# Adding the output projection to x with ScalarE and POOL instead of VectorE in a four-layer RWKV and graph-convolution kernel

## The chip, the cores and the metric

The kernel runs on one core of a Trainium2 chip. The metric is the device time of one execution, in microseconds (us). A profile is one execution recorded by the hardware profiler; its span is the time from the first to the last recorded instruction. Engines are named as in the profile: PE is TensorE (matrix products), DVE is VectorE, ACT is ScalarE, POOL is GpSimd, and SP is SyncE, whose queue issues the large transfers between HBM and SBUF here.

## The reference

x has 16 images of 192 channels and 56 x 56 points, in fp32. Three layers of a bidirectional RWKV mixer and one graph convolution follow each other, each on a group-normalised x and each added to x:

```
for layer in 0, 1, 2:                     # T = 3136 points, C = 192 channels
    xs = group_norm(x)                    # 32 groups, over 6 channels and all points
    k, v, r = xs @ Wk.T, xs @ Wv.T, xs @ Wr.T
    x_bi = 0.5 * (wkv(k, v) + flip(wkv(flip(k), flip(v))))
    h = sigmoid(r) * x_bi
    h = (h - mean(h)) * rsqrt(var(h) + 1e-5) * ln_g + ln_b     # over the channels
    x = x + h @ Wo.T
x_j = max(0, x shifted by 2 points in each of four directions, less x)      # on group_norm(x)
x = x + gelu(batch_norm([x, x_j] @ conv_w.T + conv_b))
```

wkv is a scan over the points: per channel, p becomes decay * p + exp(k) * v and q becomes decay * q + exp(k), and the output is (p + c * exp(k) * v) / (q + c * exp(k)). The group norm of the next layer needs the sum and the sum of squares of the new x over all points, before the first product of that layer.

## The kernel before, in words

Two images make a pair: 2 x 192 channels stand in three columns j = 0, 2, 1 of 128 partitions. A tile of one chunk is 128 x 3 x 448 (448 of the 3136 points, so 7 chunks). There are eight pairs in two streams of four. While one stream runs its backward scan and its output (the functions `b_...`), the other runs the forward scan of its layer (`a_...`) or the graph convolution (`c_...`). A table of 249 steps says which units meet: `both_a` (85 steps) and `both_a_first` (17) join a backward chunk b with a forward chunk a, `both_c` (42) a backward chunk with a convolution chunk, `forward_a` (66), `forward_c` (14), `backward_alone` (24) and `neither` (1) have one or none.

There is no scheduler: within a step each function writes its instructions, and each engine carries out its own in the order in which they were written. `nback` and `nfront` are the chunks of the next step, whose r and k products and exponentials are begun a step early. The output of a backward chunk is spread over two or three steps: `late` holds the chunks that are not finished and how far they are, and l is such a chunk.

One chunk of `both_a` in its parts, with the lines of the profile:

- `b_q`, `b_p`, `a_q`, `a_p`: three scans each on VectorE (L836). Their decays lie in PSUM. `save` copies the last column for the next chunk, q's on ACT (L845), p's on POOL (L847).
- `b_den`, `b_num`, `a_den`, `a_num`: the bonus c * exp(k) added to the state, two VectorE operations each (L851), both inputs in SBUF.
- `a_ekv`: exp(k) * v from v's product in PSUM (L885). `b_scale`: h times the inverse deviation from PSUM (L1014). `b_rs2`: the variance (L997).
- `invert`: 1 / q as exp(-ln q) on ACT (L906, L909); `b_sigmoid` likewise (L941, L909); `b_exp`, `a_exp` (L934, L866) take the exponentials out of PSUM.
- `b_mix`: nine POOL operations (L969 to L971) that form h. `a_y`: one POOL product over the whole chunk (L913), into the tile that the backward pass of that layer adds to.
- `b_squares` (L978), `b_sums` (PE, `st`), `b_rs1`, `b_rs3` (L993, L1002, L1003), `b_spread` (PE, `rsb`): the deviation over the channels.
- `b_out`: the output product, `ops` in PSUM. `b_x`: adds it and a column `wob` to x in SBUF, three VectorE operations (L1027), and sends x to HBM through SP's queue (L1029).
- `b_stats`, called by `sum_up`: per column j one pass on ACT for the sum and one for the sum of squares of the new x (L722, L723). With the last chunk (c = 0) the next layer begins: its `norm_sums` (L728), `norm_var` and `norm_fold` come at the next calls of `gap()`.

PSUM has seven banks for products, taken and returned in turn (`bank`, `release`); a product waits until the last reader of its banks is done. SBUF has 33 chunk slots, also taken in turn. SP's queue carries, in the written order, the loads of the next chunks (`load_ahead`), the stores of the convolution's result (`store`) and the stores of x.

Of the kernel before, what the change touches and what calls it, by code (L numbers as in the profile page):

```python
# [39 lines left out]
P = 128  # L40
# [433 lines left out]
def fast_path(ctx: ExitStack, tc: tile.TileContext, flag, x, wproj, wfold, wcfold, wconst, wgroup, sums, picks, vecs, out):  # L474
# [7 lines left out]
    keep = ctx.enter_context(tc.tile_pool(name="fkeep", bufs=1))  # L482
    row = ctx.enter_context(tc.tile_pool(name="frow", bufs=1))
    small = ctx.enter_context(tc.tile_pool(name="fsmall", bufs=4))
    dram = ctx.enter_context(tc.tile_pool(name="fdram", bufs=1, space=bass.MemoryType.DRAM))
    psum = ctx.enter_context(tc.tile_pool(name="fpsum", bufs=1, space=bass.MemoryType.PSUM))
    psconst = ctx.enter_context(tc.tile_pool(name="fpsconst", bufs=1, space=bass.MemoryType.PSUM))
# [217 lines left out]
    class Run:  # L705
        def __init__(self, pr, l, stats, src=None, first=None):
            self.pr, self.l, self.stats, self.src = pr, l, stats, src
            self.xa, self.xb, self.xz = {}, {}, {}
            if first is not None:
                self.xa[0] = first  # L710
            self.begun = False
            self.bias, self.carry, self.ps = {}, {}, {}
            self.ek, self.ekv, self.h, self.den, self.sg, self.rs = {}, {}, {}, {}, {}, {}
            self.m, self.ml, self.q, self.p = {}, {}, {}, {}

    def new_stats():
        return small.tile([P, 2, 3, NL], F32, tag="stats", name=name("stats"))

    def chunk_stats(stats, xt, c):

        for j in ORDER:
            S.activation(junk, xt[:, j, :], AF.Identity, accum_out=stats[:, 0, j, c : c + 1])  # L722
            S.activation(junk, xt[:, j, :], AF.Square, accum_out=stats[:, 1, j, c : c + 1])  # L723


# [115 lines left out]
    def save(run, key, s, col, eng=G):  # L841

        run.carry[key] = stile("c" + key)
        if key == "q":
            S.activation(run.carry[key], s.t[:, :, col : col + 1], AF.Copy)  # L845
        else:
            eng.tensor_copy(run.carry[key], s.t[:, :, col : col + 1])  # L847
# [167 lines left out]
            release(ps[j])  # L1015

    def b_out(run, c):
        h = run.h.pop(c)
        run.ps["o"] = banks("ops")
        project(run.ps["o"], params[run.l][5], of(h.t), L)  # L1020
        h.give()

    def b_x(run, c):
        wob, ps, xs = params[run.l][4], run.ps["o"], run.xb[c]
        for j in ORDER:
            xj = xs.t[:, j, :]
            V.scalar_tensor_tensor(xj, ps[j][:, 0:L], wob[:, column(j)], xj, ALU.add, ALU.add)  # L1027
            release(ps[j])
        nc.sync.dma_start(run.dst[c], xs.t)  # L1029

    def b_stats(run, c):
        xs = run.xb.pop(c)
        chunk_stats(run.new, xs.t, c)
        if c == 0:
            require_all(run.chk, slice(0, NCHK))
            nxt = run.follow
            nxt.stats, nxt.src = run.new, run.dst
            nxt.xa[0] = xs
            begin_later(nxt)
        else:  # L1040
            xs.give()
# [135 lines left out]

    late, unsummed = {}, []  # L1180

    def of_stage(n):
# [22 lines left out]
    def add(u):  # L1205
        b_x(*u)
        unsummed.append(u)
        del late[u]

    def keys(f):  # L1210
        if f is not None:
            begin_now(f[1])
# [11 lines left out]
    def both_a(b, a, nback, nfront):  # L1224
# [5 lines left out]
        store()  # L1230
        if nback is not None:
            b_gate(*nback[1:])
            b_exp(*nback[1:])
        b_q(*b)
        if l:
            b_rs2(*l)
            b_rs3(*l)
        b_sigmoid(*b)
        a_values(*a)
        if l:  # L1240
            b_spread(*l)
        b_p(*b)
        b_den(*b)
        invert(b[0].ek[b[1]])
        b_num(*b)
        b_mix(*b)
        if l:
            b_scale(*l)
            b_out(*l)
            late[l] = 2  # L1250
        a_ekv(*a)
        sum_up()
        keys(nfront)
        a_q(*a)
        if l:
            add(l)
        b_squares(*b, (0,))
        a_save(*a)
        exp_keys(nfront, (0, 2))
        b_squares(*b, (2,))  # L1260
        exp_keys(nfront, (1,))
        b_squares(*b, (1,))
        b_sums(*b)
        a_p(*a)
        gap()
        a_den(*a)
        b_rs1(*b)
        late[b] = 0.5
        invert(den())
        gap()  # L1270
        a_num(*a)
        a_y(*a)
        gap()

    def both_a_first(b, a, nback, nfront):

# [89 lines left out]
    def forward_a(a, nback, nfront):  # L1366
# [10 lines left out]
        if l and late[l] == 0:  # L1377
            squares_and_sums(l)
            b_rs1(*l)
            late[l] = 0.5  # L1380
        if l and late[l] == 0.5:
            b_rs2(*l)
            b_rs3(*l)
            late[l] = 1
        if l:
            b_spread(*l)
        elif ahead:
            keys(nfront)
        store()
        a_q(*a)  # L1390
        a_save(*a)
        if ahead and not l:
            exp_keys(nfront)
        a_den(*a)
        gap()
        invert(den())
        a_ekv(*a)
        gap()
        if l:
            b_scale(*l)  # L1400
            if ahead:
                keys(nfront)
                exp_keys(nfront)
            b_out(*l)
            late[l] = 2
        sum_up()
        if nback is not None:
            b_gate(*nback[1:])
        a_p(*a)
        gap()  # L1410
        if l:
            add(l)
            sum_up()
        a_num(*a)
        a_y(*a)
        if nback is not None:
            b_exp(*nback[1:])
# [235 lines left out]
```

## Time and profile before

| | before |
|---|---|
| runs, median (lowest to highest) | 5382.29 us (5372.49 to 5386.76), 3 runs |
| profiled execution, its time and its span | 5382.77 and 5381.0 us |
| busy PE, DVE, ACT, POOL | 4629.7, 5014.9, 3681.2, 2770.3 us |
| mean granted clock of PE | 0.916 |

Busy is the time in which an engine carried out at least one instruction. A group's row gives the line, the operation, out<-in by tile names, the shapes, how often, the busy sum and the mean of one in nanoseconds, then the idle time just before and what ended it. A row of the timeline gives start and duration in us of like instructions in a row; a duration holds the instruction's end as well, so three scans of 1.13 us follow each other at 1.05. `L836` is line 836 of the kernel before; the changed kernel's lines are some numbers higher.

### The profile page before, as it was taken

How to read it: one execution, taken by the hardware profiler on the slowest of the kernel's cores; microseconds unless marked ns; L12 is line 12 of the kernel's file. 1: busy time of each engine (PE TensorE's matmuls, PEld its weight loads, DVE VectorE, ACT ScalarE, POOL GpSimd, SP SyncE). 2: the span in 40 equal slices, each digit the busy share in tenths (PEclk: the TensorE clock that was granted, in tenths of full speed). 3: DMA queues.
4: the chain of work that ended last, by engine and by line, in shares of the span. 5: the costliest groups of instructions: out<-in, count | busy, mean ns of one | idle time of the engine just before them, and what ended most of it. 6: DMA issues, size and time to landing. Idle time of an engine off the chain costs nothing. (4 is left out here: it accounts for less than half of the span.)

```text
span 5381.0 us, 50984 instructions
## 1 busy us (share of the span) xinstructions
PE 4629.7 (86%) x15206; PEld 1498.6 (28%) x15206; DVE 5014.9 (93%) x6556; ACT 3681.2 (68%) x7035; POOL 2770.3 (51%) x2164
## 2 busy tenths in 40 slices
PE   6888988989798898888979888888888988898897
PEld 2222322223232222222323222222222222222222
DVE  6989999999999999999999999999999999999996
ACT  6777667767676676676667767667667566676673
POOL 1555555645454465555444455555535455555463
PEclk8989989989899898998989989999898998999898
DMA  5222212124243212213425121221343312222233
GB/s 149 78 80 72 85 66 88 63 90 140 87 131 89 82 63 73 74 67 105 144 87 150 56 74 67 85 74 62 111 139 94 111 56 74 70 77 80 77 102 115
DMA packets 314271, 482.42 MB, mean 90 GB/s; under 512 B 66432, under 2 KB 306688, under 8 KB 313984
## 3 DMA queue, kind: packets, MB, share of 16 engines
q1 hardware_dynamic: 312832, 477.59, 27.9%
q8 instruction: 123, 2.02, 0.2%
q10 hardware_dynamic: 1152, 1.48, 0.1%
q14 instruction: 164, 1.34, 0.1%
HBM read 324.83 MB, written 154.14 MB: 89 GB/s over the span
## 5 line engine op out<-in xcount | busy, mean ns | idle before, releaser
L913 POOL TENSOR_TENSOR p<-p,q 128x1344 f32<-128x1344 f32 x168 | 510.1, 3037 | 887.8 <-ACT q L909 472.1
L969 POOL TENSOR_TENSOR ekv<-ekv,ek 128x448 f32<-128x448 f32 x504 | 618.2, 1227 | 677.1 <-DVE p L1014 304.9
L836 DVE TENSOR_TENSOR_SCAN p<-fdecays,cp,ekv 128x448 f32<-128x448 f32 x864 | 928.5, 1130 | 7.2 <-POOL p L913 4.5
L836 DVE TENSOR_TENSOR_SCAN q<-fdecays,cq,ek 128x448 f32<-128x448 f32 x864 | 929.2, 1131 | 1.9 <-PE st L987 0.2
L971 POOL TENSOR_TENSOR p<-p,sg 128x448 f32<-128x448 f32 x504 | 599.4, 1189 | 54.5 <-ACT cq L845 10.7
L970 POOL TENSOR_TENSOR p<-p,ekv 128x448 f32<-128x448 f32 x504 | 600.6, 1192 | 39.5
L847 POOL COPY cp<-p 128x3 f32<-128x3 f32 x271 | 196.4, 725 | 686.9 <-DVE p L836 454.3
L978 ACT ACTIVATE ek<-p 128x448 f32<-128x448 f32 x504 | 283.6, 573 | 259.4 <-POOL p L971 257.5
L591 PE MATMUL ops<-p,fwo 128*128 128x448 f32 x336 | 223.5, 755 | 275.3 <-DVE p L1014 275.2
L866 ACT ACTIVATE ek<-k,k 128x448 f32<-128x448 f32 x504 | 292.1, 630 | 243.0 <-PE k L594 216.4
L723 ACT ACTIVATE fjunk<-x 128x448 f32<-128x448 f32 x672 | 387.6, 577 | 21.1
L722 ACT ACTIVATE fjunk<-x 128x448 f32<-128x448 f32 x672 | 384.6, 572 | 14.6
L851 DVE SCALAR_TENSOR_TENSOR q<-ek,fcc,q 128x896 f32<-128x896 f32 x336 | 337.1, 1043 | 51.1 <-ACT cq L845 51.1
L1009 PE MATMUL rsb<-rs,fpicks 32*128 32x448 f32 (+1 forms) x1008 | 335.8, 594 | 48.8 <-ACT rs L1003 46.7
L1027 DVE SCALAR_TENSOR_TENSOR x<-ops,fwob,x 128x448 f32<-128x448 f32 x504 | 315.9, 674 | 52.2 <-PE ops L594 27.1
L851 DVE SCALAR_TENSOR_TENSOR ek<-ek,fcc,q 128x896 f32<-128x896 f32 x336 | 361.6, 1117 | 2.8 <-POOL chk L919 2.8
L851 DVE SCALAR_TENSOR_TENSOR ekv<-ekv,fcc,p 128x896 f32<-128x896 f32 x336 | 330.4, 1024 | 1.2
L934 ACT ACTIVATE sg<-r,r 128x448 f32<-128x448 f32 x504 | 311.9, 624 | 15.8 <-PE r L594 10.4
L885 DVE SCALAR_TENSOR_TENSOR ekv<-v,v,ek 128x448 f32<-128x448 f32 x504 | 312.9, 677 | 0.0
L1014 DVE TENSOR_TENSOR p<-p,rsb 128x448 f32<-128x448 f32 x504 | 281.5, 614 | 31.1 <-PE rsb L1009 31.0
L851 DVE SCALAR_TENSOR_TENSOR p<-ekv,fcc,p 128x896 f32<-128x896 f32 x336 | 293.4, 913 | 10.0 <-POOL cp L847 9.7
L906 ACT ACTIVATE q<-q 128x1344 f32<-128x1344 f32 x168 | 222.4, 1324 | 90.4 <-DVE q L851 65.9
(232 smaller groups left out, 11795.3 us busy)
## 6 DMA issues: line engine op xcount, KB each, us to landing
x<-xd SPq DMA_DIRECT2D x240, 672.0 KB, 5.5
xd<-x SPq DMA_DIRECT2D x168, 672.0 KB, 4.0
x<-in_x_dram SPq DMA_DIRECT2D x320, 224.0 KB, 4.6
x<-in_x_dram SPq DMA_DIRECT2D x320, 112.0 KB, 4.6
out_dram<-ml SPq DMA_DIRECT2D x112, 224.0 KB, 2.3
ring<-xd SPq DMA_DIRECT2D x112, 168.0 KB, 5.3
wkv<-in_wfold_dram SPq DMA_DIRECT2D x24, 640.0 KB, 5.5
out_dram<-ml SPq DMA_DIRECT2D x112, 112.0 KB, 2.3
```

What stands on the lines that cost most here:

```text
L722: S.activation(junk, xt[:, j, :], AF.Identity, accum_out=stats[:, 0, j, c : c + 1])
L723: S.activation(junk, xt[:, j, :], AF.Square, accum_out=stats[:, 1, j, c : c + 1])
L836: V.tensor_tensor_scan(s.t[:, j, order], dec[:, column(j)].to_broadcast([P, L]), data.t[:, j, order], init, ALU.mult, ALU.add)
L851: by_channel(lambda js, i: V.scalar_tensor_tensor(dst.t[:, js, :], e.t[:, js, :], cc[:, i : i + 1], state.t[:, js, :], ALU.mult, ALU.add))
L885: V.scalar_tensor_tensor(e.t[:, j, :], ps[j][:, 0:L], b[:, j, :], run.ek[c].t[:, j, :], ALU.add, ALU.mult)
L913: G.tensor_mul(run.h[c].t, run.h[c].t, den.t)
L934: S.activation(sg.t[:, j, :], ps[j][:, 0:L], AF.Exp, bias=b[:, j, :], scale=-1.0, accum_out=run.chk[:, at : at + 1])
L969: G.tensor_mul(y.t[:, j, :], y.t[:, j, :], den.t[:, j, :])
L970: G.tensor_add(h.t[:, j, :], h.t[:, j, :], y.t[:, j, :])
L971: G.tensor_mul(h.t[:, j, :], h.t[:, j, :], sg.t[:, j, :])
L1009: PE.matmul(ps[j][:, :L], pick[rows, j, :], rs[rows, :], start=True, stop=True)
L1027: V.scalar_tensor_tensor(xj, ps[j][:, 0:L], wob[:, column(j)], xj, ALU.add, ALU.add)
```

## The change

In `both_a`, the output product of chunk l is no longer added to x by VectorE. ACT reads it from PSUM, adds `wob`, writes it over h and sums it by its accumulator (`b_evict`); POOL then adds h to x (`b_add`), behind `a_y`. As the accumulated sum is that of the addend alone, `whole_sums` adds the old x's sums, once for each run. Wherever VectorE still adds (`b_x`, all other steps), its operation writes the sum by an accumulator. So the pass for sums on ACT is gone everywhere and `b_stats` takes only squares. In `both_a` the state of p of chunk a is copied by ACT, the k product of the next chunk stands ahead of the output product, and `b_exp`, `a_q`, `a_ekv`, the squares and the Ln and Exp of den change places. `forward_a` with a chunk left over is put in another order too, with the output product ahead of k and `add` behind `a_num`. The statistics tiles get a pool of their own with seven buffers.

```diff
-    def chunk_stats(stats, xt, c):
-
-        for j in ORDER:
             S.activation(junk, xt[:, j, :], AF.Identity, accum_out=stats[:, 0, j, c : c + 1])
+        chunk_squares(stats, xt, c)
+
+    def chunk_squares(stats, xt, c):
+        for j in ORDER:
             S.activation(junk, xt[:, j, :], AF.Square, accum_out=stats[:, 1, j, c : c + 1])
...
-        if key == "q":
+        if key == "q" or eng is S:
             S.activation(run.carry[key], s.t[:, :, col : col + 1], AF.Copy)
...
     def b_x(run, c):
+        run.h.pop(c).give()
         wob, ps, xs = params[run.l][4], run.ps["o"], run.xb[c]
         for j in ORDER:
             xj = xs.t[:, j, :]
-            V.scalar_tensor_tensor(xj, ps[j][:, 0:L], wob[:, column(j)], xj, ALU.add, ALU.add)
+            V.scalar_tensor_tensor(
+                xj, ps[j][:, 0:L], wob[:, column(j)], xj, ALU.add, ALU.add, accum_out=run.new[:, 0, j, c : c + 1]
+            )
             release(ps[j])
         nc.sync.dma_start(run.dst[c], xs.t)
+    def b_evict(run, c):
+        wob, ps, h = params[run.l][4], run.ps["o"], run.h[c].t
+        for j in ORDER:
+            S.activation(
+                h[:, j, :], ps[j][:, 0:L], AF.Identity, bias=wob[:, column(j)], accum_out=run.new[:, 0, j, c : c + 1]
+            )
+            release(ps[j])
+    def b_add(run, c):
+        h, xs = run.h.pop(c), run.xb[c]
+        G.tensor_add(xs.t, xs.t, h.t)
+        h.give()
+        nc.sync.dma_start(run.dst[c], xs.t)
+        run.parts.append(c)
+    def whole_sums(run):
+        if run.parts:
+            cs = slice(min(run.parts), max(run.parts) + 1)
+            new = run.new[:, 0, :, cs]
+            G.tensor_add(new, new, run.stats[:, 0, :, cs])
     def b_stats(run, c):
         xs = run.xb.pop(c)
-        chunk_stats(run.new, xs.t, c)
+        chunk_squares(run.new, xs.t, c)
         if c == 0:
+            whole_sums(run)
...
     def both_a(b, a, nback, nfront):
         if nback is not None:
             b_gate(*nback[1:])
-            b_exp(*nback[1:])
         b_q(*b)
...
         invert(b[0].ek[b[1]])
+        if nback is not None:
+            b_exp(*nback[1:])
+        b_spread(*l)
         b_num(*b)
         b_mix(*b)
-        if l:
-            b_scale(*l)
-            b_out(*l)
-            late[l] = 2
+        a_q(*a)
+        a_save(*a)
         a_ekv(*a)
+        b_squares(*b, (0,))
         sum_up()
         keys(nfront)
-        a_q(*a)
-        if l:
-            add(l)
-        b_squares(*b, (0,))
-        a_save(*a)
-        exp_keys(nfront, (0, 2))
+        b_scale(*l)
+        b_out(*l)
         b_squares(*b, (2,))
-        exp_keys(nfront, (1,))
+        exp_keys(nfront)
+        a_p(*a, S)
         b_squares(*b, (1,))
-        b_sums(*b)
-        a_p(*a)
         gap()
         a_den(*a)
-        b_rs1(*b)
-        late[b] = 0.5
-        invert(den())
+        ln(den())
         gap()
         a_num(*a)
+        exp_minus(den())
+        b_sums(*b)
+        b_rs1(*b)
+        b_evict(*l)
         a_y(*a)
+        add_evicted(l)
         gap()
+        late[b] = 0.5
...
     def forward_a(a, nback, nfront):
+            b_spread(*l)
+            a_den(*a)
+            invert(den())
+            sum_up()
+            a_ekv(*a)
             b_scale(*l)
+            b_out(*l)
+            if nback is not None:
+                b_gate(*nback[1:])
             if ahead:
                 keys(nfront)
                 exp_keys(nfront)
-            b_out(*l)
-            late[l] = 2
-        sum_up()
-        if nback is not None:
-            b_gate(*nback[1:])
-        a_p(*a)
-        gap()
-        if l:
+            a_p(*a)
+            a_num(*a)
             add(l)
             sum_up()
```

## The prediction

> **What bounds the kernel now.** I read the busy table first, then the groups, then one step in the timeline, engine by engine.
>
> ```profile
> span 5381.0 us, 50984 instructions
> ...
> PE 4629.7 (86%) x15206; PEld 1498.6 (28%) x15206; DVE 5014.9 (93%) x6556; ACT 3681.2 (68%) x7035; POOL 2770.3 (51%) x2164
> ```
>
> VectorE (DVE) is nearly full, but that is a mean over seven kinds of step. Placing every instruction in its step (the program's order against the trace's, starts of VectorE's first instruction), the span holds 85 `both_a` steps (2171 us), 42 `both_c` (1045), 43 `forward_a` with no chunk left over (566), 17 `both_a_first` (507), 23 `forward_a` with one left over (449), 24 `backward_alone` (364) and others (213). The change acts on `both_a` first. They come in 17 rows of five, each row behind a `both_a_first`. Busy times of two neighbouring `both_a` steps (window, its length, then PE, PEld, DVE, ACT, POOL with counts, PE's granted clock, DMA share, GB/s), and from the timeline VectorE and POOL in the first (start, us, instruction):
>
> ```profile
> 426.59:451.91 25.32, 23.75 (x79) 7.52 (x78) 25.26 (x31) 19.13 (x36) 15.21 (x12) 0.93 0.27 83
> 451.91:477.23 25.32, 22.43 (x79) 6.94 (x78) 25.26 (x31) 19.18 (x36) 15.20 (x12) 1.00 0.23 81
> ```
>
> ```profile
> 433.65 1.72 DVE L851 SCALAR_TENSOR_TENSOR ek<-ek,fcc,q 128x896 f32<-128x896 f32 x2
> 435.29 1.74 DVE L851 SCALAR_TENSOR_TENSOR ekv<-ekv,fcc,p 128x896 f32<-128x896 f32 x2
> ...
> 443.46 1.84 DVE L1027 SCALAR_TENSOR_TENSOR x<-ops,fwob,x 128x448 f32<-128x448 f32 x3
> 445.22 3.23 DVE L836 TENSOR_TENSOR_SCAN p<-fdecays,cp,ekv 128x448 f32<-128x448 f32 x3
> 448.36 1.98 DVE L851 SCALAR_TENSOR_TENSOR q<-ek,fcc,q 128x896 f32<-128x896 f32 x2
> 450.25 1.74 DVE L851 SCALAR_TENSOR_TENSOR p<-ekv,fcc,p 128x896 f32<-128x896 f32 x2
> ```
>
> ```profile
> 428.56 3.04 POOL L913 TENSOR_TENSOR p<-p,q 128x1344 f32<-128x1344 f32 x1 [4.11 <-ACT q L909]
> ...
> 447.64 1.15 POOL L971 TENSOR_TENSOR p<-p,sg 128x448 f32<-128x448 f32 x1
> 448.73 1.06 POOL L847 COPY cp<-p 128x3 f32<-128x3 f32 x1
> 453.82 3.04 POOL L913 TENSOR_TENSOR p<-p,q 128x1344 f32<-128x1344 f32 x1 [4.03 <-ACT q L909]
> ```
>
> A step takes 25.32 us; VectorE works 25.26 of it, without a gap. But PE is at 22.4 us with the clock at 1.00 and 23.75 at 0.93, so it is close behind. ACT has 6 us to spare, POOL 10. And POOL's idle time is not free time. In a later `forward_a`, POOL's product and VectorE's two-input operation meet:
>
> ```profile
> 530.93 3.03 POOL L913 TENSOR_TENSOR p<-p,q 128x1344 f32<-128x1344 f32 x1 [5.11 <-ACT q L909]
> ...
> 532.36 3.15 DVE L851 SCALAR_TENSOR_TENSOR q<-ek,fcc,q 128x896 f32<-128x896 f32 x2 [0.32 <-ACT cq L845]
> ```
>
> The pair takes 1.72 us alone and 3.15 here: the 1.43 us more is the wait from 532.36 to about 0.2 before POOL's end at 533.96. The scans keep 1.13 us each under POOL's work.
>
> **What the skill says.** "SBUF — State Buffer", section "Who interferes with whom": a VectorE instruction with two SBUF inputs and a POOL instruction that reads SBUF exclude each other for the whole instruction, while one with a single SBUF input doesn't contend. The trace agrees (1.43 us above; `decays` is in PSUM, so a scan has one). "GPSIMD Engine Reference", "Engine selection": two-input elementwise work is about 2x slower there; the trace has 3.04 us on POOL against 1.6 on VectorE for 1344 columns (L1067). "TensorE: Matmul & The Clock Gate", Part 1: PE drops to half clock after an idle window of about 3.4 us; the trace has 0.93 and 1.00 in neighbouring steps. "VectorE: DVE Perf Modes", "Two Vector instructions with no wait between them": an operation with an accumulator output is two instructions; no row of this kernel has one on VectorE.
>
> **`both_a`, 85 steps.** VectorE loses L1027, 3 x 0.59 = 1.76 us from start to start, and the 0.25 us that `q` (1.98, not 1.72) waited for POOL: 25.3 - 2.0 = 23.3 us. ACT loses three sum passes (0.70 from start to start, 2.1 us) and gains three evictions (PSUM to SBUF with accumulator, as L934: 0.62 to 0.75, about 2.1 us) and one copy (0.2): nothing in sum, but the evictions stand at its tail and end about 4.1 us into the next step. Behind them on ACT wait the copy of q's state, rs3 and the sigmoid (0.2 + 1.3 + 2.7, until 8.3); Ln of ek is due at 8.8, so 0.5 us covers them, and each us beyond it would count in full. `b_exp`, moved behind Ln and Exp of ek, frees r's banks at 13.6 for rsb and k; `b_scale` wants rsb at 15.4: covered by 1 us. POOL loses one copy (1.06, mostly a wait) and gains one addition of 128x1344, taken as L913's 3.04 (L1094, the same form, has 3.17).
>
> Behind the addition on POOL stand the next copy of p and the mix at 11.6 us: not late. `whole_sums`, one small POOL operation in each of 24 runs (0.2 us by its 128x3 product, L919), ends long before `mv` is read, and the larger statistics pool moves no work: nothing for either.
>
> Now the order. The addition stands after L913, which waits for exp(-ln den), which is queued on ACT behind the last square, which waits for POOL's mix. Follow it with the trace's times from `b_den` at 433.65: `b_den`, Ln and Exp of ek, nine mix operations until 448.79: 15.14 us; square 0.61 (ends 449.40); Ln and Exp of den 2.71; hand-over and L913 0.14 + 3.04; addition 3.04, less 0.2 for the early release: 24.5 us. What comes then is the next step's `b_den`, which has two SBUF inputs and waits. On top of it, `a_den` now reaches VectorE 1.76 us earlier, at 20.0 us of the step, while the mix runs until 22.2: the last mix operation lets half of `a_den` (1.06) pass first and starts 0.7 to 1.0 later, and VectorE itself waits twice, 0.7 to 0.9 each. So a loop of 25.2 to 25.5 us takes the place of VectorE's 23.3.
>
> Two more loops end close by. PE: k 4.6, output product 4.6, st 2.2 (which formerly was not behind it), then rs1 0.6, rs2 0.65, `b_p` 3.15, two bonuses 3.3, `a_q` 3.15, two of `a_ekv` 1.2, which frees k's banks, and hand-overs 0.3: 23.7 us, with half clock in part of it (each such window costs 1.7) about 24.7. I also see PE left with only the short rsb products between v and k for some 4 us, no better than now for the clock. SP: the store now waits for the addition at 7.4 us of the next step, and that step's loads stand behind it in SP's queue:
>
> ```profile
> 445.33 0.56 SPq L1029 DMA_DIRECT2D xd<-x  x1
> 446.00 0.56 SPq L540 DMA_DIRECT2D x<-in_x_dram  x1
> ...
> 448.99 0.57 SPq L545 DMA_DIRECT2D x<-xd  x1
> ```
>
> Today they leave 18.7 us into the step before the one that uses them. After: 7.4 + 0.67 (store) + 0.67 (load for b) + 5.5 (median landing) = 14.2 us, against k's start at 14.9: hidden. In layer 0, b's load is four transfers (446.00 to 448.99, 3 us): 16.6 us, 1.7 late.
>
> The first `both_a` of a row of five has no addition ahead of it: 23.3 and the two waits at `a_den`, 24.7 to 24.8, -0.6. The other four: the first loop's middle, 25.35, and an estimated 0.2 for steps where half clock makes PE's loop the longer one: 25.55, +0.25 each (rounded up). Five steps: +0.4 us; x 12 rows = +5. Four layer-0 rows have about 2 late steps, +3.5 in all: 4 x 3.9 = +16. The row that also sums the input (28 to 29 us, ACT's chain, same load): 0.
>
> **`forward_a` with a chunk left over, then `backward_alone`.** 17 pairs follow a `both_a`. Loss: L913 and then the addition stand in front of `a_den`, which moved ahead: VectorE waits 0.1 + 2.9 us instead of 1.43; the output product starts 1.1 later than today. Gain: the next run's `mv` (VectorE waits 3.15 us for it until 553.8 in the first such step of layer 1) needs three passes on ACT after the last x, not six: -2.1. Net -1.0 x 17 = -17 us. The other six: 0.
>
> **Accumulators on VectorE.** The 83 chunks still added there get 249 reads. Nearest rows: VectorE's 128x1 and 128x3 copies, 0.065 to 0.2 from start to start; ACT's accumulator read, 0.19 a row. I take 0.15, bounds 0.05 and 0.3; no gain is possible from an added instruction. On the path: `both_c` (35 adds) and `both_a_first` (17), full of VectorE work: 156 x 0.15 = 23; `forward_a`, where VectorE waits for the product anyway (1.03 and 0.69), 5: +28 us (9 to 56). ACT's saved passes in `both_c` lie beside a gapless VectorE: 0; were they on its path, -2.1 x 35.
>
> **Sum.** +5 + 16 - 17 + 28 = +32 us on a span of 5381.0; that execution took 5382.77, the median of the runs is 5382.29: **5414 us**.
>
> **Rivals.**
> (B) The relief arrives: 24.3 us a step, VectorE's 23.3 and 1.0 of stalls. It decides if L913 and the addition are over when `b_den` comes at 7.05 us, that is, if exp(-ln den) ends by 0.95 + 0.2 us of the next step; by my loop it is 1.3, so 0.2 us a step decides, and a mix that starts 0.3 earlier would do it. For it: POOL's 10 idle us. Against: the chain above. 80 x -1.0 - 17 + 15 = -82: 5300 us.
> (C) SP's queue or the clock takes over: loads late in every row (landing 7 us instead of 5.5) or half clock in k's product each step: +0.9 x 68 + 16 + 28 - 17 = +88: 5470 us.
> (D) The parts cancel, reads at 0.05 and rows of layer 0 unharmed: +5 + 0 - 17 + 9 = -3: 5379 us, no change; what a measurement can tell here is about 0.3%, 16 us.
>
> **Chances.** Mine 0.45, B 0.25, C 0.14, D 0.16. Mine alone: 5390 to 5445 (reads 9 to 56, rows). The range 5310 to 5480 reaches into B and C until 2 in 10 are left out. Faster by over 0.3%: B and a tail of D, 0.28; within: 0.16; slower: 0.56.
>
> **What would show it.** Right: `both_a` steps of 25.2 to 25.8 us with VectorE gaps or stretched L851 rows (over 1.5 us in `ek` and `q`), the addition's row ending at 7 to 8 us of the next step, `mv` idle near 1 us. Wrong: `ek` rows of 1.13 us and steps under 24.5 (B); k's product waiting for a DMA in all rows (C); accumulator reads that fill no time. The weakest step is the loop of 25.2 to 25.5: 1% of it is 20 us.

## The result and the profile after

The changed kernel takes 5499.51 us (median; 5498.14 to 5501.03) against 5380.74 us before (5372.49 to 5386.76): a ratio of 1.0222, 95% interval 1.0204 to 1.024. The forecast was 5414 us, slower; the sign was right, but the loss is 119 us where 32 were forecast, and the time lies outside the range of 5310 to 5480.

The head of the changed kernel's page (span, then busy time, its share and the number of instructions of each engine):

```profile
span 5498.3 us, 50732 instructions
...
PE 4765.6 (87%) x15206; PEld 1535.6 (28%) x15206; DVE 5082.7 (92%) x6550; ACT 3516.2 (64%) x6622; POOL 3020.9 (55%) x2181
```

PE carries out the same 15206 products and is busy 136 us longer; its mean granted clock fell from 0.916 to 0.889. VectorE has lost 255 additions (and has 249 short accumulator reads more) and is busy 68 us longer too. Both did less or the same work and took more time for it, which points to waiting inside instructions (VectorE) and a slower clock (PE).

Two neighbouring `both_a` steps, the same two in the order of the program as those from 837 to 888 us before, which take 25.3 each (window, its length, busy PE, PEld, VectorE, ACT, POOL with counts, clock, DMA share, GB/s):

```profile
856.68:883.79 27.11, 25.82 (x80) 8.08 (x78) 25.99 (x29) 19.13 (x36) 17.94 (x12) 0.87 0.22 77
883.79:910.89 27.10, 25.81 (x80) 8.09 (x78) 25.99 (x28) 19.11 (x36) 17.96 (x12) 0.87 0.15 51
```

27.1 us, and no engine is full. I placed every instruction in its step, as in the prediction. Changes in us over all steps of a kind: `both_a` +117, `forward_a` with a chunk left over +25, other `forward_a` +12, `both_c` +9, `backward_alone` -44, `neither` -2, others 0; the sum is the +117 of the spans. Of the five `both_a` steps in a row the first takes 24.97 us and the other four 27.11, 133.4 us together, 126.7 before.

VectorE in the first of the two steps, from the timeline (start, us, instruction, idle time before and what ended it):

```profile
860.99 0.63 DVE L1003 TENSOR_TENSOR rs<-st,rs 64x448 f32<-64x448 f32 x1 [1.08 <-ACT rs L999]
...
864.80 2.80 DVE L857 SCALAR_TENSOR_TENSOR ek<-ek,fcc,q 128x896 f32<-128x896 f32 x2
867.52 1.73 DVE L857 SCALAR_TENSOR_TENSOR ekv<-ekv,fcc,p 128x896 f32<-128x896 f32 x2
...
878.84 3.36 DVE L857 SCALAR_TENSOR_TENSOR q<-ek,fcc,q 128x896 f32<-128x896 f32 x2
```

and POOL beside it:

```profile
858.09 3.05 POOL L919 TENSOR_TENSOR p<-p,q 128x1344 f32<-128x1344 f32 x1 [3.50 <-ACT q L915]
863.01 3.04 POOL L1050 TENSOR_TENSOR x<-x,p 128x1344 f32<-128x1344 f32 x1 [1.88 <-ACT p L1043]
...
879.85 1.87 POOL L977 TENSOR_TENSOR p<-p,sg 128x448 f32<-128x448 f32 x1
```

Three losses stand in these rows. `b_den` (the `ek` row) takes 2.80 us instead of 1.72: POOL's addition, 863.01 to 866.05, holds it up for 1.08. `a_den` (the `q` row) takes 3.36 instead of 1.98 and the mix operation beside it 1.87 instead of 1.13: they stop each other. And `b_rs2` (the `rs` row) waits 1.08 for `b_rs1`. Beyond the 1.72 us that each pair takes alone they come to 1.08 + 1.64 + 1.08 = 3.8 us, and 27.1 less 3.8 is 23.3: the prediction had VectorE's own work right. But the addition doesn't follow L919 at once, as the prediction had it: it waits 1.88 us for ACT's evictions. ACT at the end of the step:

```profile
883.80 1.32 ACT L915 ACTIVATE q<-q 128x1344 f32<-128x1344 f32 x1
887.52 0.54 ACT L999 ACTIVATE rs<-st 64x448 f32<-64x448 f32 x1 [2.40 <-PE st L993]
888.09 0.63 ACT L1043 ACTIVATE p<-ops,fwob 128x448 f32<-128x448 f32 x1
...
889.32 0.63 ACT L1043 ACTIVATE p<-ops,fwob 128x448 f32<-128x448 f32 x1
```

ACT is done with exp(-ln den) at 885.1 and then stands for 2.40 us at `b_rs1`, with the evictions queued behind. It waits for `st`, the last product of the step in PE's queue, and PE is late:

```profile
869.29 1.01 PE L1015 MATMUL rsb<-rs,fpicks 32*128 32x448 f32 x2
871.59 3.53 PE L1015 MATMUL rsb<-rs,fpicks 32*128 32x448 f32 x4 [1.29 <-ACT sg L940]
875.05 1.86 PE L592 MATMUL k<-x,wkv 128*128 128x448 f32 x2
...
881.24 1.02 PE L592 MATMUL ops<-p,fwo 128*128 128x448 f32 x2
...
886.91 0.55 PE L993 MATMUL st<-ek,fsums 128*32 128x448 f32 x2
```

The first third of rsb is done at 870.3; the rest waits until `b_exp` has read r's banks, and is then carried out at half clock, as is part of k: k starts at 875.05 and takes 6.2 us instead of 4.6. Half clock (the records grant PE 0.5 of full speed) is granted for 7.7 us of a mean `both_a` step, 4.0 before. The group of rsb over the whole kernel, before and after (busy us, mean ns, idle before):

```profile
L1009 PE MATMUL rsb<-rs,fpicks 64*128 64x448 f32 x336 | 174.7, 601 | 0.0
L1009 PE MATMUL rsb<-rs,fpicks 32*128 32x448 f32 x672 | 173.0, 591 | 48.8 <-ACT rs L1003 46.7
```

```profile
L1015 PE MATMUL rsb<-rs,fpicks 32*128 32x448 f32 x672 | 282.1, 654 | 181.5 <-ACT sg L940 172.4 <-ACT rs L1009 8.6
L1015 PE MATMUL rsb<-rs,fpicks 64*128 64x448 f32 x336 | 229.7, 773 | 0.0
```

So a ring is closed that the prediction didn't have as a whole: `b_den`, Ln and Exp of ek, `b_exp`, rsb, k, output product, `st`, `b_rs1`, evictions, addition, and the next `b_den`. From this `b_den` to the next each link starts within 0.2 us of the end of the one before, so the ring has no slack: its length is the step. The experiments ask which of its links cost how much.

### The profile page after: what moved, and what is told of

It reads as the page before. It is cut to its first block, busy times and chain, and to the rows that moved or that the text cites. A ratio compares the mean times of both kernels' runs of the same rounds, so it can differ in the third digit from the quotient of the medians.

```text
span 5498.3 us, 50732 instructions
## 1 busy us (share of the span) xinstructions
PE 4765.6 (87%) x15206; PEld 1535.6 (28%) x15206; DVE 5082.7 (92%) x6550; ACT 3516.2 (64%) x6622; POOL 3020.9 (55%) x2181
## 5 line engine op out<-in xcount | busy, mean ns | idle before, releaser
L919 POOL TENSOR_TENSOR p<-p,q 128x1344 f32<-128x1344 f32 x168 | 511.3, 3043 | 705.4 <-ACT q L915 414.8
L977 POOL TENSOR_TENSOR p<-p,sg 128x448 f32<-128x448 f32 x504 | 659.6, 1309 | 43.2 <-ACT sg L915 4.0
L1015 PE MATMUL rsb<-rs,fpicks 32*128 32x448 f32 (+1 forms) x1008 | 500.0, 694 | 181.5 <-ACT sg L940 172.4
L857 DVE SCALAR_TENSOR_TENSOR q<-ek,fcc,q 128x896 f32<-128x896 f32 x336 | 481.7, 1473 | 58.6 <-ACT cq L851 58.0
L853 POOL COPY cp<-p 128x3 f32<-128x3 f32 x186 | 110.5, 594 | 632.6 <-DVE p L842 353.3
L857 DVE SCALAR_TENSOR_TENSOR ek<-ek,fcc,q 128x896 f32<-128x896 f32 x336 | 429.5, 1317 | 2.8 <-POOL chk L925 2.8
L729 ACT ACTIVATE fjunk<-x 128x448 f32<-128x448 f32 x672 | 385.2, 573 | 17.6 <-issue 1.2
L1050 POOL TENSOR_TENSOR x<-x,p 128x1344 f32<-128x1344 f32 x85 | 272.4, 3204 | 126.8 <-ACT p L1043 72.7
L592 PE MATMUL k<-x,wkv 128*128 128x448 f32 (+1 forms) x336 | 242.9, 816 | 95.3 <-DMA x<-xd 88.2
L592 PE MATMUL ops<-p,fwo 128*128 128x448 f32 x336 | 200.5, 683 | 112.6 <-DVE p L1020 112.4
```

The costliest lines, as they stand in the source:

```text
L592: PE.matmul(ps[0][:, :n], w(0, 0), r(slice(0, P), 0), start=start, stop=False)
L857: by_channel(lambda js, i: V.scalar_tensor_tensor(dst.t[:, js, :], e.t[:, js, :], cc[:, i : i + 1], state.t[:, js, :], ALU.mult, ALU.add))
L919: G.tensor_mul(run.h[c].t, run.h[c].t, den.t)
L977: G.tensor_mul(h.t[:, j, :], h.t[:, j, :], sg.t[:, j, :])
L1015: PE.matmul(ps[j][:, :L], pick[rows, j, :], rs[rows, :], start=True, stop=True)
```

## Experiments

Means of a step by kind in the profiled execution, in us, placed as above; "late" is `forward_a` with a chunk left over, "half" the half clock in a mean `both_a` step. `before` and `after` are medians of four executions; other times without a range are one execution each (two executions of a kernel here differ by up to 0.3%, 16 us).

| kernel | time | both_a | late | both_c | half |
|---|---|---|---|---|---|
| before | 5380.7 | 25.54 | 19.50 | 24.88 | 4.0 |
| after | 5499.5 | 26.92 | 20.57 | 25.10 | 7.7 |
| e1 part of v's product twice | 5437.5 | 26.08 | 20.85 | 25.14 | 4.0 |
| e2 no addition | 5363.6 | 25.86 | 19.22 | 25.16 | 6.5 |
| e3 b_exp moved up | 5454.8 | 26.18 | 21.03 | 25.25 | 6.2 |
| e4 accumulators alone | 5321.3 (5319.9 to 5323.1) | 25.55 | 19.85 | 24.68 | 4.0 |
| e5 e1 and e2 | 5330.6 | 25.52 | 18.85 | 25.28 | 3.6 |
| e6 old forward_a | 5477.5 | 26.86 | 21.05 | 25.08 | 7.6 |
| e7 e4, addition moved, old order | 5535.9 | 26.96 | 22.89 | 25.44 | 7.1 |
| e8 e4, p's state copied by ACT | 5321.2 (5319.4 to 5322.1) | 25.59 | 19.70 | 24.68 | 4.2 |
| e9 evictions ahead of b_rs1 | 5416.5 | 25.87 | 20.75 | 25.26 | 6.1 |
| e10 h's slot returned early | 5481.7 | 26.79 | 20.84 | 24.70 | 7.6 |
| e11 e9, store on POOL's queue | 5415.7 | 25.87 | 20.75 | 25.27 | 5.9 |
| e12 e6, e9, e10 together | 5396.8 (5395.6 to 5403.2) | 25.97 | 21.74 | 24.67 | 6.6 |
| e13 e12, VectorE adds in a row's last step | 5404.8 | 26.31 | 20.61 | 24.64 | 6.8 |
| e14 e12 and e1 | 5373.8 | 25.71 | 21.26 | 24.66 | 4.0 |
| e15 e4, new order of both_a | 5511.6 | 27.49 | 21.04 | 24.71 | 7.6 |
| e16 e12, b_exp moved up | 5421.3 | 26.07 | 21.88 | 24.68 | 5.8 |
| e17 e16, store on POOL's queue | 5429.1 | 26.03 | 22.58 | 24.65 | 5.8 |
| e18 e17, a_ekv ahead of a_q | 5399.4 | 25.88 | 21.88 | 24.71 | 3.2 |

### The clock and the addition, each by itself (e1, e2, e3, e5)

e1, on the changed kernel, with 6 of v's 14 product instructions carried out a second time, which changes no result:

```diff
         b_sigmoid(*b)
+        xs = a[0].xa[a[1]]
         a_values(*a)
+        project_rest(a[0].ps["v"][1], a[0].w[1], of(xs.t), L)
```

> The changed kernel, with the last three matrix products of v (its column j = 1) carried out a second time in both_a, right behind v: 2.0 us more PE work per step in the time in which PE waits for r's banks; the result is the same. Clock theory (b_exp, moved behind Ln and Exp of ek, keeps r's banks until 15 us, rsb is cut in two, PE idles and runs at half clock for 6.8 us of every step, so k, the output product, st and rs1 come late): half clock under 4 us per step, both_a steps of 25.3 to 26.2 instead of 27.1, in all 5400 to 5450. Lock theory (the step is set by POOL's addition holding up b_den, whatever PE does): steps of 27.1 or more, 5500 to 5520.

e2 leaves out POOL's addition, so x isn't the reference's:

```diff
         h, xs = run.h.pop(c), run.xb[c]
-        G.tensor_add(xs.t, xs.t, h.t)
         h.give()
```

> The changed kernel without POOL's addition of h to x in both_a (it leaves those 85 chunks of the output product out of x; all other work, evictions, stores and waits stay). Lock theory: b_den no longer waits, and the step falls to VectorE's own 23.3 us and the two waits at a_den, 24.8; forward_a loses 2.9: in all about 5290. Clock theory: b_den's 1.08 us go, but PE's half clock of 6.8 us stays, since r's banks are held as long as before; the step is then PE's chain through rs1 and rs2, 26.0 to 26.2: in all 5380 to 5430.

e3 puts `b_exp` in the sigmoid's place and the sigmoid behind Ln and Exp of ek:

```diff
         b_rs3(*l)
-        b_sigmoid(*b)
+        if nback is not None:
+            b_exp(*nback[1:])
         a_values(*a)
...
         invert(b[0].ek[b[1]])
-        if nback is not None:
-            b_exp(*nback[1:])
+        b_sigmoid(*b)
```

> The changed kernel with b_exp ahead of Ln and Exp of ek (behind rs3) and the sigmoid behind them, so that r's banks come free at about 8 us. Clock theory: rsb runs in one piece right behind v, half clock falls to 2 us a step or less, k is held by a_ekv alone, steps of 25.2 to 25.7: 5370 to 5420. Lock theory: the addition still ends at 9 us of the next step and b_den waits as now: 26.5 to 27.1, 5460 to 5500.

e5 has the edits of e1 and e2:

> Of the changed kernel POOL's addition is left out (so x isn't the reference's) and the second part of v's product is carried out twice, which keeps PE at full clock. The clock alone took both_a from 26.92 to 26.08 us, the addition alone to 25.86. Theory that these are two causes that add up: both_a at 25.0 us or below, 5290 us. Rival, one cause that either edit breaks (or a third, such as the loads behind the store, that bounds the step next): both_a stays at 25.7 to 26.0 us, 5355 to 5370 us.

e1 came out as the clock theory had it; e2 and e5 lie between their two ranges and e3 outside both. e1 brings the half clock back to the 4.0 us of the kernel before, not to nothing. Either edit alone takes about 1 us off the mean step (26.92 to 26.08, to 25.86). With both it is 25.52, held up by the first row of layer 0 (27 to 30 us a step), each row's second step (26.1) and most first steps (25.5); the third to fifth run at 24.97. So both causes are real. They aren't independent in each step: in e1 some steps run at 25.0 and some stay at 27.1. In e3 rsb is in one piece (1.97 us), but k then waits for x's load (203 us over 60 waits, 88 in the changed kernel) and for v's banks (93), and the half clock stays at 6.2: moving one link of PE's chain only shows the next.

The 24.97 us is a second finding. Two such steps of e5 by window:

```profile
832.25:857.22 24.97, 24.96 (x96) 7.81 (x88) 24.91 (x28) 19.59 (x38) 14.92 (x11) 1.00 0.31 100
857.22:882.18 24.96, 24.41 (x92) 7.68 (x84) 24.90 (x28) 19.01 (x37) 14.93 (x11) 1.00 0.18 56
```

With full clock and no addition VectorE is still full, 24.91 of 24.97. (PE, with the six extra instructions, is as full; but the first step of a row in the changed kernel, without them, takes the same 24.97.) Its `q` row takes 3.40 us there, 1.68 more than the pair alone: `a_den`, 1.8 us earlier than before, now falls into the mix. So of the 2.0 us by which the prediction shortened VectorE's step, only 0.35 (25.32 to 24.97) could be had in this order.

### The accumulators, and p's state (e4, e8)

e4 is the kernel before with the accumulators alone, VectorE adding everywhere:

```diff
     def b_x(run, c):
...
-            V.scalar_tensor_tensor(xj, ps[j][:, 0:L], wob[:, column(j)], xj, ALU.add, ALU.add)
+            V.scalar_tensor_tensor(
+                xj, ps[j][:, 0:L], wob[:, column(j)], xj, ALU.add, ALU.add, accum_out=run.new[:, 0, j, c : c + 1]
+            )
...
-        chunk_stats(run.new, xs.t, c)
+        chunk_squares(run.new, xs.t, c)
```

> The kernel before with one part of the change: sums of x from an accumulator of VectorE's addition, for all 168 chunks, and no pass for sums on ACT. My prediction's 0.15 us for each of 504 reads: +50 to +75 us less 2.1 us at 17 layer starts (-36), 5395 to 5420. From the rows of the changed kernel (80 ns, the next operation starts 0.60 us after the last as without it): no cost, and the layer starts gain 2.1 to 2.7 us each: 5335 to 5350.

e8 adds one more edit to e4 (`save` takes the engine, as in the change):

```diff
-        a_p(*a)
+        a_p(*a, S)
```

> The accumulators alone (5321 us) and, on top, the last column of p copied by ACT instead of POOL in both_a: VectorE's q bonus no longer waits 0.25 us for POOL's copy. If VectorE is what bounds these steps: 85 x -0.25 = -21 us, 5300 us, both_a 25.3 us. Rival, the wait only moves to PE or POOL, or the copy on ACT delays Ln of den: both_a stays at 25.5, 5321 us.

e4 takes 5321.33 us, a ratio of 0.9887 (0.987 to 0.9903): 59 us faster than before, faster than both kernels of this case and than either expectation. The accumulator read has a row of its own, but fills no time of VectorE's. From e4's timeline (a group's first number is its start):

```profile
847.32 0.66 DVE L1031 SCALAR_TENSOR_TENSOR x<-ops,fwob,x 128x448 f32<-128x448 f32 x1
847.90 0.09 DVE L1031 DVE_READ_ACCUMULATOR x<-ops,fwob,x 128x1 f32 x1
847.90 0.68 DVE L1031 SCALAR_TENSOR_TENSOR x<-ops,fwob,x 128x448 f32<-128x448 f32 x1
848.51 0.08 DVE L1031 DVE_READ_ACCUMULATOR x<-ops,fwob,x 128x1 f32 x1
```

From one addition to the next it is 0.58 and 0.61 us, 0.58 and 0.59 in the kernel before: the read lies under the next operation. Over all neighbouring additions the median goes from 0.592 to 0.604 us, about 0.01 us a read. The gain is the saved passes: VectorE's waits for `mv` fall from 77.5 to 34.7 us, `backward_alone` steps from 15.18 to 13.09 (24 of them, -50 us).

e8 changes nothing (0.9893, 0.9876 to 0.9909). The `q` row is 1.94 us with POOL's copy (e4) and 1.93 without (e8): what holds it is the last mix operation, which ends at 22.2 us of the step. The expectation had taken the copy for it.

### The move and the order, each alone (e7, e15, e6)

e7 is e4 with the addition moved and nothing else in `both_a`. Outside it, h's slot is returned as late as in the changed kernel (see e10):

```diff
-        if l:
-            add(l)
...
         a_num(*a)
+        b_evict(*l)
         a_y(*a)
+        add_evicted(l)
```

> The accumulators alone (5321 us) and, on top, the addition moved to ACT and POOL, with every other operation in its old place. Lock theory (the addition behind POOL's last product reaches into the next step and holds up b_den): both_a 25.5 to 26.2 us, ek bonus rows of 1.6 us or more, 5320 to 5380 us. Order theory (the new order of k, b_exp, a_q and the squares costs, the addition's move by itself gives VectorE's 2 us back): both_a at most 24.7 us, 5260 us or less.

e15 has the new order of `both_a` and the copy by ACT, but VectorE adds, at the end of its step, since the output product comes late in this order (`forward_a` in the old order, h's slot returned early):

```diff
         a_num(*a)
+        add(l)
         exp_minus(den())
         b_sums(*b)
         b_rs1(*b)
-        b_evict(*l)
         a_y(*a)
-        add_evicted(l)
```

> The accumulators and the new order of both_a (k ahead of the output product, b_exp behind Ln and Exp of ek, p's state copied by ACT), but VectorE adds, after its last operation of the step; forward_a in the old order. If the new order costs by itself (rsb behind b_exp, half clock in k): both_a 25.8 us or more instead of 25.55, 5345 us or more. If it costs only together with the addition: both_a at most 25.5 us, 5300 to 5325 us.

e6 is the changed kernel with the old text of `forward_a`:

> The changed kernel, with the old order in forward_a alone. If the new order of forward_a costs by itself (steps with a chunk left over 20.57 instead of 19.85 us, and the plain forward_a steps after them 13.45 instead of 12.91): both return to these, about -17 and -23 us: 5460 us. If the lateness is handed over by both_a, whose addition still runs when forward_a begins: both stay, 5490 to 5500 us.

Both expectations that excused one half fell; e7 lies above both of its ranges. The move alone costs 215 us on top of e4, the order alone 190, both (e6) 156. In `both_c`, which neither half touches, 32 of e7's 215 and 17 of e6's 156 arise, against 1 in e15, which returns h's slot early; so that much is more likely the slots' (e10) than the move's. In e7 the addition comes last on POOL, in the next step, and `b_den` waits for it (POOL, then VectorE):

```profile
898.02 3.05 POOL L1050 TENSOR_TENSOR x<-x,p 128x1344 f32<-128x1344 f32 x1
```

```profile
898.73 3.88 DVE L857 SCALAR_TENSOR_TENSOR ek<-ek,fcc,q 128x896 f32<-128x896 f32 x2
```

2.16 us of waiting in a row that takes 1.72 alone; the step is 27.3 us. In e15 there is no addition on POOL, and the step is 27.4 all the same:

```profile
876.64 3.25 DVE L857 SCALAR_TENSOR_TENSOR q<-ek,fcc,q 128x896 f32<-128x896 f32 x2
...
883.35 0.69 DVE L1034 SCALAR_TENSOR_TENSOR x<-ops,fwob,x 128x448 f32<-128x448 f32 x1 [0.57 <-PE ops L601]
```

VectorE stops 1.5 us in `a_den`, and PE, with rsb cut and 7.6 us of half clock, is so late that VectorE waits for the last third of the output product. Each half by itself makes `both_a` steps of about 27 us, so they don't add up: whoever undoes one still has the other.

e6 is 22 us faster than the changed kernel. In the first plain `forward_a` after a convolution row the new order has k behind the output product; the step takes 19.9 us, 16.1 with the old order, six times over (-23 us). The steps with a chunk left over don't return to 19.85; they rise to 21.05.

### What makes the addition late, and two smaller causes (e9 to e12)

e9 changes one place on ACT:

```diff
-        b_rs1(*b)
         b_evict(*l)
+        b_rs1(*b)
```

> The changed kernel with b_evict ahead of b_rs1 on ACT. In the changed kernel ACT stands idle for 2.4 us before rs1, waiting for st from PE, and the evictions and then the addition stand behind it. If that queue is what makes the addition late: evictions end before rs1, the addition follows POOL's product at once, 1.8 us earlier, the ek bonus row falls from 2.2 to under 1.3 us and the step from 27.1 to about 26.0 us: 68 x -1.05 = -71, 5428 us. Rival, PE's loop with its half clock bounds the step by itself and the lock only fills time that is free: both_a stays at 26.7 to 27.0, 5480 to 5500 us.

e10 returns h's slot at the output product again, save in `both_a`:

```diff
-    def b_out(run, c):
+    def b_out(run, c, keep=False):
         run.ps["o"] = banks("ops")
         project(run.ps["o"], params[run.l][5], of(run.h[c].t), L)
+        if not keep:
+            run.h.pop(c).give()
```

> The changed kernel with h's slot returned at the output product, as before, wherever VectorE still adds (in both_a the addition needs it longer). Slot theory: the later return shifts the turn in which chunk slots are handed out, so that in the second both_c step of a row m and ml get slots whose last readers on POOL and ACT aren't done (25.9 us instead of 23.25, VectorE waits 2.0 and 2.5 us): 7 rows x -2.65 = -19, 5480 us. Rival, the waits come with the accumulators or the order of the steps before: no change, 5499 us.

e11 is e9 with `nc.gpsimd.dma_start` for the store in `b_add`:

> As the run with b_evict ahead of b_rs1 (forecast 5428 us), with the store of the added x sent from POOL's own queue instead of SP's, so that no load stands behind it. If the late loads cost: PE's 88 us of waits for x before k nearly vanish, the first row of layer 0 (27 to 31 us a step) is 1 to 2 us shorter a step, 10 to 30 us below the run it builds on. Rival, POOL's issue of the store (about 1 us of an engine that is in the loop) costs as much: within 10 us of it or above.

e12 has e6, e9 and e10 together:

> b_evict ahead of b_rs1, h's slot returned early wherever VectorE adds, and the old order of forward_a, together in the changed kernel. If the three parts are separate and add up: 5499 - 71 - 19 - 22 = 5387 us. If they hide one another: 5410 us or more. Either way above the 5321 us of the accumulators alone, since both_a still has rsb behind b_exp, the clock's half windows and the two stops at a_den.

e9 gives 83 us back with two lines exchanged. The addition now follows L919, and `b_den` is free of it (POOL, then VectorE):

```profile
837.08 3.04 POOL L919 TENSOR_TENSOR p<-p,q 128x1344 f32<-128x1344 f32 x1 [3.27 <-ACT q L915]
840.09 3.03 POOL L1050 TENSOR_TENSOR x<-x,p 128x1344 f32<-128x1344 f32 x1
```

```profile
843.25 1.72 DVE L857 SCALAR_TENSOR_TENSOR ek<-ek,fcc,q 128x896 f32<-128x896 f32 x2
```

Steps alternate between 25.3 and 26.3 us. e10 gives 18 us: with the later return the slots come round in another turn, and in the second `both_c` step of a row `ml` gets one that ACT still reads (three rows) or a store still sends (four). The changed kernel:

```profile
1487.44 0.51 DVE L1084 TENSOR_TENSOR m<-ring,x 128x336 f32<-128x336 f32 x1 [1.95 <-POOL ml L1127]
...
1491.59 0.59 DVE L1096 TENSOR_TENSOR ml<-x 128x416 f32<-128x416 f32 x1 [2.45 <-ACT fjunk L729]
```

In e10 the first of these waits is still there, inside the row (2.34 us for 0.51); the second, 2.45 us, is gone, and the step is back at 23.25. The expectation had counted both. e11 gains nothing: k no longer waits for x's load (73 us in e9), but waits 96 us for v's banks instead. e12 doesn't reach the sum of its parts (5376 from 5499.5 less 83, 22 and 18): 5397, a ratio to before of 1.0036 (1.0022 to 1.005). Against e4 it lacks 76 us; by the steps 36 in `both_a` and 44 in `forward_a` with a chunk left over, the rest near nothing.

### What is left (e13, e14, e16, e17, e18)

e13 is e12 with VectorE's addition in the last `both_a` step of a row (`add(l)` ahead of `b_rs1` where b is chunk 0):

> The run with three parts undone (5397 us) and, on top, VectorE adds the output product in the last both_a step of each row, so that no addition of POOL reaches into forward_a. If that addition (it holds up the first two-input operations of forward_a) costs the 44 us: forward_a with a chunk left over falls from 21.74 to about 20.0 us, the last both_a step grows by 0.5, 5397 - 31 + 8 = 5374 us. Rival, forward_a is late for another reason (half clock, r's product): 21.5 us or more stays, 5395 us or more.

e14 is e12 with the edit of e1:

> The run with three parts undone (5397 us) and, on top, the second part of v's product carried out twice, which keeps PE at full clock. If the alternation of 25.3 and 26.3 us in both_a follows the half-clock windows: steps of 25.0 to 25.3 us, 85 x -0.65 = -55, 5342 us. Rival, the addition alone makes it (it still ends after b_den can start): 25.9 us stays, 5385 us or more.

e16 is e12 with the edit of e3:

> The run with three parts undone (5397 us) and, on top, b_exp ahead of the sigmoid, as in the earlier run. If rsb's wait for r's banks (150 us in 68 steps) sets PE's loop: both_a at 25.3 us, half clock under 5 us a step, 5397 - 50 = 5347 us. Rival, k then waits for v's banks (freed by a_ekv) or for x's load instead, and the half clock stays: both_a 25.8 us or more, 5380 to 5400 us.

e17 is e16 with e11's store:

> The same, with the store sent from POOL's queue, so that the loads of x don't stand behind it. If x's load is what k waits for once rsb is early: 20 us or more below the run with the store in SP's queue, k's waits for x nearly gone. If a_ekv, which frees v's banks, is: within 10 us of it, with k waiting for ekv instead.

e18 is e17 with `a_ekv` ahead of `a_q`:

> The run with b_exp early and the store on POOL's queue (5429 us, both_a 26.03), with a_ekv ahead of a_q. If the turn of the seven PSUM banks is what keeps PE waiting: k follows rsb within 1 us, half clock falls under 4 us a step, both_a 25.0 to 25.3 us, 5429 - 70 = 5360 us. If PE is not what bounds the step any more: half clock falls too, but both_a stays at 25.8 us or more, 5410 us or more.

All five gave less than hoped. e13: the late steps fall by 1.13 us, 26 in all, so the last addition is more than half of the 44, but the step in which VectorE adds grows by about 2 us and takes it back. e14: 23 us of 55; 45 of 85 steps at 25.3, most second steps still at 26.3. e16 and e17: nothing gained, they are 24 and 32 us slower than e12. With rsb early, k stands before the next bank; the line of PE's waits in e17 (us in all, times, longest):

```profile
PE k L593 <- DVE ekv L891: 310.7, 85, 6.7
```

PSUM's seven banks go round, and each product waits for the readers of the one before last; `a_ekv`, behind `a_q`, gives v's banks back at 15.7 us of the step. e18 takes most of that away: k waits 105 us for v's banks instead of 311, half clock is down to 3.2 us, and the steps stand at 25.95 all the same:

```profile
835.87:861.82 25.95, 22.70 (x80) 6.85 (x78) 24.99 (x29) 18.89 (x37) 18.38 (x13) 0.99 0.19 64
```

```profile
840.01 0.63 DVE L1003 TENSOR_TENSOR rs<-st,rs 64x448 f32<-64x448 f32 x1 [0.93 <-ACT rs L999]
...
856.76 2.60 DVE L857 SCALAR_TENSOR_TENSOR q<-ek,fcc,q 128x896 f32<-128x896 f32 x2
859.28 2.61 DVE L857 SCALAR_TENSOR_TENSOR p<-ekv,fcc,p 128x896 f32<-128x896 f32 x2
```

PE, busy 22.70 of 25.95 us, isn't the bound here. What is left, as I read the trace (no run breaks this loop), is the loop through POOL's mix: `a_den` and `a_num` lose 0.88 and 0.87 us to the mix and the mix 0.95 and 0.26 to them, its square and Ln and Exp of den come later, the three evictions (1.9 us) stand ahead of `b_rs1`, and `b_rs2` waits 0.93 for it in front of the next `b_p` and `b_den`.

## Why the prediction was wrong

**The step that failed is the term of `both_a`: +5 and +16 forecast, +117 measured.** Its loops were sized one by one, "25.2 to 25.5" for the addition and "about 24.7" for PE, and the longer one taken; the trace shows one ring of 27.1 through both. Two of its numbers were wrong:

- PE. `b_exp` at 13.6 us frees r's banks "for rsb and k", rsb is wanted at 15.4: "covered by 1 us". In the trace `b_exp` frees the last bank that rsb needs at 14.9, the rest of rsb takes 3.5 us at half clock, and rsb is complete at 18.4. The clock was written down as a loss of 1.7 us for each half-clock window, in part of the steps; it is 6.8 us at half clock, a loss of 3.4, in every steady step. PE's `st` ends 30.8 us after the step's start.
- ACT. The evictions "end about 4.1 us into the next step". They end at 6.2, because `b_rs1`, which waits for that `st`, stands ahead of them. The addition ends at 9.4, not at 7.4, and costs `b_den` 1.08 us. The prediction's chain let the addition follow L913 directly; e9, where it does, has 25.3 to 26.3 us a step. That is what the forecast's loop describes, and its mean of 25.87 is 0.3 above the 25.55.

So the two loops were one ring: PE's delay reaches POOL through ACT's queue. Three edits at three of its links (PE in e1, POOL in e2, ACT in e9) each shorten the mean step, by 0.84, 1.06 and 1.05 us. Rival C, "half clock in k's product each step" (5470 us), is the nearest of those written down; its price of 0.9 us a step ended at PE and was too low.

**First step of a row**: 24.97 against 24.7 to 24.8; the two stops at `a_den` cost 1.68 us (e5). That lies within the prediction's own "0.7 to 0.9 each", of which its sum took only the low end. This also ends rival B for this order: its 24.3 us a step was not to be had, as e5 shows.

**Layer 0**: of four later rows of layer 0 three are 1.4 us longer than others and one 0.2, 4.5 in all where 14 were forecast beyond the general +0.4; the row that also sums the input is 5.9 us longer than before, not 0. The loads behind the store, forecast as hidden outside layer 0, delay k in the last step of 16 of the 17 rows, in every layer, by 5.2 to 5.6 us (86 of 88 us); the early steps of layer 0's rows have only four short waits (2.5 us). But e11 shows that without them the next wait stands in the same place, and the time stays.

**`forward_a` and `backward_alone`**: forecast -17 for the 17 pairs, measured -16, in part by luck: +1.6 us each in `forward_a` and -2.6 in `backward_alone`, where +1.1 and -2.1 were forecast, two errors of 0.5 that cancel. The other six were put at 0: there the steps with a chunk left over gain 0.6 us each, but the plain `forward_a` behind them loses up to 3.8 by the new order, +12 over all, which the prediction didn't look at (e6).

**Accumulators**: +28 forecast; e4 shows no loss. 0.15 us for a read was the mis-sized term: about 0.01 was measured, below its lower bound of 0.05. The "accumulator reads that fill no time" were among the prediction's own signs of being wrong. And in `both_c` the turn of the slots (+18 in e10) was missing altogether; it hides the accumulators' gain there.

Do rsb's 32- and 64-row products or the idle 1.3 us between them bring the half clock on? e16 doesn't tell: it leaves 5.8 us with rsb in one piece, but with a longer idle time behind it. The traces tell more. In them the clock changes in multiples of 3.41 us. In the window from 868.34 PE is busy for 62%, but for 36% if each product counts by the share of the 128 rows that it uses, and half clock follows. In the next, from 871.75, PE is busy all the time, 41% by rows, and half clock stays; in the one from 875.16 it is 100% by both, and full clock follows. I counted such windows in all 20 traces, with limits set after looking. At full clock and with PE busy for 62 to 85%, those under 46% by rows are followed by half clock in 383 of 399 cases, those of 50% or more in 4 of 1377. At half clock and with PE busy for 90% or more, those under 80% by rows are followed by half clock in all 422 cases, those of 85% or more in 195 of 3164. So with the same busy time it is the few rows that go with the half clock; no run was made to test it. The runs don't say where the remaining 18 us of the late steps in e12 come from.

## What to carry to other kernels

An instruction that is moved to an idle engine still has a place in that engine's queue: ask what stands ahead of it, what that waits for, and follow the chain round until it comes back to the first engine; here exchanging two lines on ACT was worth 83 of 119 us. When a busy engine is relieved, everything behind the relief moves earlier and may run into a lock that it used to miss: 1.4 of the 1.8 us of additions taken from VectorE went this way. Try the parts of a large change one at a time: the smallest part alone (the accumulators) gave 59 us, and the rest cost 178.

## What the runs showed of the hardware

- A VectorE operation with an accumulator output is two instructions in the trace, as the Trainium skill has it ("VectorE: DVE Perf Modes", "Two Vector instructions with no wait between them"), but the read of 80 ns lies almost wholly beside the next operation here: 0.604 us from addition to addition with it, 0.592 without (medians of e4 and of the kernel before). On ACT the read (0.19 us) is hidden in the same way: evictions, 0.63 us each, start every 0.61 to 0.63 us.
- The exclusion of VectorE and POOL works in both directions within one pair. In the changed kernel `a_den` waits, and the mix operation that follows then waits for it (1.87 us for 1.13); in e18 VectorE loses 0.88 and 0.87 us in such meetings and POOL 0.95 and 0.26.
- In these traces the clock goes with the rows that PE's products use, not with busy time alone: of the full-clock windows above, all busy for 62 to 85%, half clock followed 383 of 399 with few rows and 4 of 1377 with more.
- An rsb product of 64 rows takes 601 ns on average before and 773 after, on the same operands, since 139 of 336 begin at half clock, 7 before.
